# Two attention layers on eight images: the first layer's output projection cut in halves twice and moved behind the next image's queries

## The chip, the cores and the metric

The kernel runs on one core of one Trainium2 chip. The metric is the device time of one execution in microseconds, as the median of several runs. A core has five engines that run side by side, each with its own queue of instructions: TensorE (PE; its weight loads are shown apart as PEld), VectorE (DVE), ScalarE (ACT), GpSimd (POOL) and SyncE (SP), which here does nothing but issue transfers (DMAs) between the chip's DRAM and the on-chip memory, SBUF. TensorE writes its products to another memory, PSUM, from which DVE or ACT must carry them to SBUF ("evict" them). Semaphores hold an instruction until what it needs is there; an engine's queue is worked off strictly in order.

## What is computed

Eight images `x` of 512 channels and 1024 points (32 x 32) go through two attention layers, all in float32. Cut to what matters:

```python
# layer 0: group norm in 32 groups, 8 heads of 64 channels
h = group_norm(x)
q, k, v = split(w_qkv @ h + b_qkv)                 # per head: 64 x 1024 each
weight = softmax((q * s).T @ (k * s))              # s = 64 ** -0.25
a = weight @ v                                     # 512 x 1024
x = x + (w_proj @ a + b_proj)                      # the projection and its residual
# layer 1: group norm in 8 groups, one head of 512 channels
xn = group_norm(x)
q, k, v = q_w @ xn + q_b, k_w @ xn + k_b, v_w @ xn + v_b
attn = softmax(q.T @ k / sqrt(512))
out = x + (p_w @ (attn @ v) + p_b)
```

## The kernel before

**Tiles.** Channels lie on 128 partitions, so an image is four tiles of 128 x 1024. All such tiles (4 KB in each partition) come from one pool, `big`, of `NBIG` = 32; `wpool` holds three sets of weights, loaded a product or two ahead by `load_weight` (line 320) in the order of the list `uses`.

**Fewer multiplications.** A 512 x 512 weight times an image is done as a 2 x 2 block product with seven block products in place of eight (the Winograd form of Strassen's method); this is "in halves once" (`wino`, line 225): sums and differences of the halves of the weights are made in the prologue and kept in DRAM (`prepare`, `keep`), those of the image by `image_factors` (line 343, eight DVE instructions of 128 x 512). "In halves twice" (`conv2`, line 501) does each of the seven block products in seven smaller ones. It needs the weight's inner sums (`keep2`, line 294) and the image's (`inner_factors`, line 403: for each of seven factors four GpSimd subtractions of 128 x 256, in the order of `ORDER`). `conv2` is written as four `pair`s of block products, (1, 5), (2, 6), (7) and (3, 4). Behind each pair the functions in a list of "hooks" are called: this is how other work is placed in the order of the program. The last two steps of a product are put into `tail` and emitted behind the first step of the next one.

**Who uses which.** Values, keys and queries of layer 0 (`values`, `keys_and_queries`) and layer 1's first product (`layer1_scores`, weight "m") are in halves twice; the projection of layer 0 (`projection`, line 954, weight "p") and layer 1's "z" product are in halves once. In `projection` DVE adds bias and residual while it evicts (line 964), half tile by half tile, then the statistics of layer 1's norm are taken (`GroupNorm.half_stats`, line 90) and the result is stored to DRAM (`store`, `spills`).

**The loop** (line 1055) runs over the images b. `attention0` (line 632) has eight blocks, four head pairs `hp` by two halves of the queries `tb`: in each, eight times two score matmuls (`sc`), an exponential on ACT (`e`), DVE adds up the eight exponentials (lines 653 and 655), then 16 matmuls with the values (`av`). Behind each head pair `reciprocals` (line 586) adds the totals over the partitions with TensorE (`sums`), sends them through DRAM and back as a broadcast `r`, by which the result `a` is scaled (line 684) during a later block. The list `extra` has 16 entries, one behind each block's scores and one behind its `av`: work for other engines is hung there. Before the change these are the loads' norm of layer 1 for the image before (`applies`), its halvings, and the halvings of `a`. Then follow the projection of image b, layer 1 of image b - 1 (`layer1_scores`, `layer1_rest`), and the values, keys and queries of image b + 1. The first image has no layer 1 to do yet, the last has no next image.

**Order.** The tile framework orders each engine's instructions by when it reckons them ready, earlier ones in the program first; an instruction given to `tc.keep_in_program_order` stays behind the one traced before it on its engine. All matmuls are pinned in this way, so TensorE works in the order of the program. Other instructions that are ready early may be put ahead.

Of the kernel before, what the change touches and what calls it, by code (L numbers as in the profile page):

```python
# [15 lines left out]
P = 128  # L16
EPS = 1e-5
ORDER = (1, 5, 2, 6, 7, 3, 4)
NBIG = 32
# [10 lines left out]
def two_attention_blocks_kernel(  # L30
# [22 lines left out]
    ident = const.tile([P, P], F32, name="ident")  # L53
    make_identity(nc, ident)
    ones = const.tile([P, P], F32, name="ones")
# [115 lines left out]
    def main_path(ctx):  # L171
# [7 lines left out]
        taken = []  # L179
        spool = ctx.enter_context(tc.tile_pool(name="spill", bufs=2, space=bass.MemoryType.DRAM))  # L180
# [111 lines left out]
        wdram2 = {n: dram.tile([P, 7, 7, P], F32, name=f"sums2_{n}") for n in "qkmv"}  # L292
# [21 lines left out]
        uses = ["p", *layer0] if B > 1 else ["p"]  # L314
        for b in range(1, B):
            uses += ["p", *twice["m"], "z"] + (layer0 if b + 1 < B else [])
# [86 lines left out]
        def inner_factors(hf, uid, pin=lambda ins: ins):  # L403

            f, steps = {}, []
            for p in ORDER:
                t = big_tile(f"inner{p}_{uid}", (P, 4, 2 * P))
                t1, t2, t3, t4 = (t[:, i, :] for i in range(4))
                b11, b12, b21, b22 = (hf[p][k][:, ts(i, 2 * P)] for k in range(2) for i in range(2))
                f[p] = {1: b11, 2: b21, 3: b22, 4: t4, 5: t1, 6: t2, 7: t3}  # L410

                def make(ops=((t1, b12, b11), (t2, b22, t1), (t3, b22, b12), (t4, b21, t2))):
                    for dst, x, y in ops:
                        pin(nc.gpsimd.tensor_tensor(dst, x, y, ALU.subtract))  # L414

                steps.append(make)
            return f, steps
# [168 lines left out]
        def reciprocals(totals, uid, across, direct=None):  # L586
# [8 lines left out]
            for t in range(n):  # L595
                for i in range(4):
                    matmul(
                        sums[ts(i, 32), t, :, :], ones[:, :32], totals[t][:, :, ts(i, P)],
                        start=t == 0, stop=t == n - 1, skip_group_check=True,
                    )  # L600
# [31 lines left out]
        def attention0(b, q, k, v, a, extra):  # L632
            n = 0
            scaled, totals = [], []

            for hp in range(KC):
                for tb in (0, 1) if hp < KC - 1 else (1, 0):
# [35 lines left out]
                    if hp < KC - 1:  # L673
                        if tb == 0:
                            continue
                        dst = a[hp].rearrange("p (t n) -> p t n", t=2)
                    else:
                        dst = dst.rearrange("p (t n) -> p t n", t=1)
                    r = reciprocals(totals, uid, False, nc.scalar if (hp, tb) == (KC - 1, 0) else None)
                    totals = []  # L680
                    engine = nc.gpsimd if (b == 0 or hp == KC - 1) and (hp, tb) != (KC - 1, 0) else nc.vector
                    scaled = [
                        lambda dst=dst, r=r, engine=engine: tc.keep_in_program_order(
                            engine.tensor_tensor(dst, dst, r, ALU.mult)  # L684
                        )
                    ]

            assert not extra
            return scaled[0]
# [118 lines left out]

        def natural(wt, nm, banks):
            ts_ = [pair_tile(f"nat{nm}_{h}") for h in range(2)]  # L810
            t = [ts_[o // 2][:, o % 2, :] for o in range(KC)]
            pt = [ps_tile(banks[o // 2], f"tr_w{nm}_{o}") for o in range(KC)]
            for kc in range(KC):
                for o in range(KC):
                    transpose(pt[o][:, ts(kc, P)], wt[kc][:, ts(o, P)], ident)
            spread(lambda o, copy: tc.keep_in_program_order(copy(t[o], pt[o])), KC)
            return t
# [34 lines left out]
        def prologue():  # L852
            raw_k = raw("k", 5)
# [46 lines left out]
            for n in "pz":  # L900
                t, steps = prepare(n)
                later.append(steps)
                later.append([lambda n=n, t=t: keep(n, t), load_weight])
# [86 lines left out]

        def norm_hooks(norm, uid):

            return [
                [], [all_background], [lambda: norm.group_mean(acc_tile(f"gmean_{uid}")[:, :KC])],
                [lambda: norm.affine(acc_tile(f"gvar_{uid}")[:, :KC])],
            ]
# [11 lines left out]
        def keys_and_queries(b, f, norm, hooks):  # L1008

            mean, affine = [], []  # L1010
            if norm:
                mean.append(lambda: norm.group_mean(acc_tile(f"gmean_0_{b + 1}")[:, :KC]))
                affine.append(lambda: norm.affine(acc_tile(f"gvar_0_{b + 1}")[:, :KC]))
            if hooks:
                k = conv2("k", f, None, f"k0_{b}", hooks)
                q = conv2("q", f, pcols("bq0"), f"q0_{b}", [[all_background], mean, affine])
            else:

                k = conv2("k", f, None, f"k0_{b}", [[all_background, *mean], [], [], affine])
                q = conv2("q", f, pcols("bq0"), f"q0_{b}")  # L1020
            return q, k

        def layer1_scores(b, inner):
            g = conv2("m", inner, ubias, f"g1_{b}")
# [29 lines left out]

        for b in range(B):
# [4 lines left out]
            h, loads, applies = [], [], []  # L1060
            if b > 0:
                h, loads, applies = begun(load_again, norm1, b - 1, "h1")
            elif B > 1:
                h, loads, applies = begun(load_x, norm0, 1, "h0")
            for f in loads:
                f()
            for i, f in enumerate(applies):
                extra[2 * i + 1].append(f)
            a = channel_tiles(f"a0_{b}")

            here = lambda *t: tc.keep_in_program_order(nc.vector.tensor_sub(*t))
            af, steps = image_factors(a, f"a_{b}", here)

            if b > 0:
                hf, t = image_factors(h, f"h1_{b - 1}", here)
                for i, fs in enumerate((t[:1], t[1:2], (t[2], t[4]), (t[6], t[3]), (t[5], t[7]), steps[:2], steps[2:4])):
                    extra[2 * i + 3] += fs
            elif B > 1:
                hf, t = image_factors(h, "h0_1", here)
                for i, fs in enumerate((t[:2], (t[2], t[4]), (t[6], t[3]), (t[5], t[7], *steps[:2]), steps[2:4])):  # L1080
                    extra[2 * i + 7] += fs
            psum_pools(f"attention_{b}", 1)
            scaled = attention0(b, q, k, v, a, extra)
            if B > 1:
                for f in steps[4:7]:
                    f()
            psum_pools(f"products_{b}", 2)
            xt = [load_x(b, c, "x") for c in range(KC)]
            if B > 1:

                inner, sums2 = inner_factors(hf, f"h1_{b - 1}" if b > 0 else "h0_1", tc.keep_in_program_order)
                for f in sums2:
                    f()
                norm1, stats = projection(b, af, xt, [scaled, steps[7]])
            if b > 0:
                gf, gsteps = layer1_scores(b - 1, inner)
                _, _, mean, affine = norm_hooks(norm1, f"1_{b}")
                if b + 1 < B:
                    h, loads, applies = begun(load_x, norm0, b + 1, "h0")
                    ahead, made = factors_ahead(h, loads, applies, f"h0_{b + 1}")  # L1100
                else:
                    h, loads, applies = begun(load_again, norm1, b, "h1")
                    ahead = [loads, *([f] for f in applies)]
                layer1_rest(b - 1, inner, gf, gsteps, stats, [[], mean, [], affine], ahead)
                if b + 1 < B:
                    v, norm0 = values(b + 1, made["inner"])
                    q, k = keys_and_queries(b + 1, made["inner"], norm0, ())
            elif B > 1:
                v, norm0 = values(1, inner)
                hooks = norm_hooks(norm1, "1_0")  # L1110
                hooks[0].append(lambda: background.extend(stats))
                q, k = keys_and_queries(1, inner, norm0, hooks)
            else:
                for f in (*steps[:7], scaled, steps[7]):
                    f()
                all_background()
                norm1, stats = projection(0, af, xt)
                finish()
                background.extend(stats)
                for f in sum(norm_hooks(norm1, "1_0"), []):  # L1120
                    f()
                h, loads, applies = begun(load_again, norm1, 0, "h1")
                for f in loads + applies:
                    f()
# [26 lines left out]
    def general_path(b, ctx):  # L1151
# [6 lines left out]
        wpool = ctx.enter_context(tc.tile_pool(name="gw", bufs=2))  # L1158

# [170 lines left out]
```

## Time and profile before

| | us |
|---|---|
| median of 3 runs (2827.34 to 2829.25) | 2828.92 |
| the profiled execution | 2828.69 |
| its span, first to last instruction | 2826.9 |
| attention of image 4 | 116.8 |
| projection of image 4 (TensorE alone on it) | 24.1 |
| one image, attention to attention | 345.4 |

The projection stands in the profile as the matmuls that write `psa_p`, `psb_p` and `psc_p`; those of the keys as `psa_k` and so on. The groups of the page that bear on the change, with busy time, mean of one, and the idle time of the engine ahead of them:

```
L651 ACT ACTIVATE e<-sc 128x1024 f32<-128x1024 f32 x512 | 476.0, 1054 | 75.8 <-PE sc L62 74.2
L414 POOL TENSOR_TENSOR inner_h<-h,inner_h 128x256 f32<-128x256 f32 x120 | 111.6, 931 | 3.5
L725 POOL TENSOR_TENSOR sum<-sum,e 128x1024 f32<-128x1024 f32 x32 | 76.1, 2378 | 27.4 <-ACT e L721 26.1
```

A matmul appears as two records. The time of a matmul is read from the distance between starts, since consecutive ones overlap. The granted clock of TensorE was 0.999 of full speed.

### The profile page before, as it was taken

Reading aid. Unit: us, or ns where it says so; the run is one execution under the profiler, and the core shown is the slowest. Engines: PE = TensorE matmul, PEld = TensorE weight load, DVE = VectorE, ACT = ScalarE, POOL = GpSimd, SP = SyncE. Lnnn points to the kernel's source line nnn. Section 1 sums busy time; section 2 is a strip of 40 time slices with the busy share of each in tenths; the row PEclk is TensorE's granted clock in tenths of the full one; section 3 lists DMA queues with packets and bytes.
Section 4 is the critical chain, followed back from the end, with each engine's and each line's share of the span. In section 5 each row is a group of like instructions: output and inputs, shape, how many; then the busy total and the mean of one; then the engine's idle time right before and its main releaser. Section 6 shows DMA issues by size and latency. Waiting matters only on the chain.

```text
span 2826.9 us, 33696 instructions
## 1 busy us (share of the span) xinstructions
PE 2808.6 (99%) x12434; PEld 1693.5 (60%) x12434; DVE 2005.0 (71%) x2833; ACT 942.7 (33%) x1205; POOL 1099.4 (39%) x1131
## 2 busy tenths in 40 slices
PE   9999999999999999999999999999999999999998
PEld 5435735866367653677537674376843868338584
DVE  5478677776777767777677766777667776676765
ACT  1252452214522145221552215422154312633130
POOL 2204205841057410664107730177202672036672
PEclk9999999999999999999999999999999999999999
DMA  8634303043031330323212232123311224112301
GB/s 285 209 114 151 147 17 127 27 174 139 24 139 52 147 129 17 139 98 120 110 50 105 101 138 90 53 102 122 140 67 53 102 112 159 36 58 90 119 5 72
DMA packets 107344, 292.41 MB, mean 103 GB/s; under 512 B 19171, under 2 KB 51235, under 8 KB 97446
## 3 DMA queue, kind: packets, MB, share of 16 engines
q1 hardware_dynamic: 105382, 287.92, 28.8%
q10 hardware_dynamic: 1792, 2.29, 0.3%
q8 instruction: 100, 1.64, 0.2%
q14 instruction: 70, 0.57, 0.1%
HBM read 237.47 MB, written 52.70 MB: 103 GB/s over the span
## 4 chain that ended last, share of the span: by engine, by line
PE 96%; DVE 2%; issue 1%; DMA 0%; POOL 0%; ACT 0%; DVEq 0%; ACTq 0%; POOLq 0%
PE sc L62 16%; PE av L62 15%; PE psb_av L62 6%; PE psb L62 5%; PE psa_av L62 4%; PE psc_av L62 4%; PE psc L62 3%; PE psa L62 3%; PE psb_z L62 3%; PE psb_k L62 3%; PE psb_g L62 3%; PE psb_v L62 3%; PE psb_p L62 3%; PE psb_q L62 2%; PE psa_z L62 2%; PE psc_z L62 2%
## 5 line engine op out<-in xcount | busy, mean ns | idle before, releaser
L655 DVE TENSOR_TENSOR sum<-sum,e 128x1024 f32<-128x1024 f32 x384 | 483.9, 1260 | 37.4 <-ACT e L651 0.5
L651 ACT ACTIVATE e<-sc 128x1024 f32<-128x1024 f32 x512 | 476.0, 1054 | 75.8 <-PE sc L62 74.2
L62 PE MATMUL sc<-q,k 64*128 64x512 f32 x2048 | 456.8, 596 | 0.0
L62 PE MATMUL av<-e,v 128*64 128x512 f32 x2048 | 453.6, 595 | 0.0
L684 POOL TENSOR_TENSOR a<-a,r 128x512 f32<-128x512 f32 (+1 forms) x11 | 20.0, 1817 | 903.3 <-DMA r<-all_rows 771.0
L62 PEld LDWEIGHTS sc<-q,k 64*128 64x128 f32 x2048 | 191.6, 186 | 248.0 <-issue 110.6
L62 PEld LDWEIGHTS av<-e,v 128*64 128x64 f32 x2048 | 141.3, 137 | 304.4 <-issue 292.3
L653 DVE TENSOR_TENSOR sum<-e,e 128x1024 f32<-128x1024 f32 x64 | 78.4, 1225 | 166.5 <-ACT e L651 166.5
L669 ACT COPY a<-av 128x512 f32<-128x512 f32 x64 | 37.5, 586 | 321.9 <-PE av L62 321.9
L62 PE MATMUL psb<-inner,inner_h 128*128 128x256 f32 x448 | 116.1, 382 | 0.9
L62 PE MATMUL psa_av<-e,z 128*128 128x512 f32 x256 | 113.3, 595 | 0.0
L414 POOL TENSOR_TENSOR inner_h<-h,inner_h 128x256 f32<-128x256 f32 x120 | 111.6, 931 | 3.5
L135 ACT ACTIVATE h<-h,b,s 128x1024 f32<-128x1024 f32 x62 | 78.5, 1270 | 87.1 <-DMA h<-in_x 69.4
L414 POOL TENSOR_TENSOR inner_h<-h 128x256 f32<-128x256 f32 x60 | 64.6, 1076 | 83.6 <-ACT h L135 83.6
L62 PEld LDWEIGHTS psb<-inner,inner_h 128*128 128x128 f32 x448 | 83.9, 190 | 16.6 <-POOL inner L429 3.5
L462 ACT COPY psb_v<-psa_v 128x512 f32<-128x512 f32 (+1 forms) x28 | 14.5, 517 | 222.4 <-DVE o L785 141.5
L725 POOL TENSOR_TENSOR sum<-sum,e 128x1024 f32<-128x1024 f32 x32 | 76.1, 2378 | 27.4 <-ACT e L721 26.1
L62 PE MATMUL psb_g<-inner_h,w_m 128*128 128x256 f32 x336 | 86.0, 383 | 0.3
L414 POOL TENSOR_TENSOR inner_h<-t_h,inner_h 128x256 f32<-128x256 f32 x90 | 84.2, 935 | 2.4
L414 POOL TENSOR_TENSOR inner_h<-t_h 128x256 f32<-128x256 f32 x90 | 79.9, 894 | 9.7 <-DVE t_h L165 9.7
L62 PEld LDWEIGHTS psa_av<-e,z 128*128 128x128 f32 x256 | 48.0, 190 | 57.3 <-issue 56.6
L721 ACT ACTIVATE e<-e 128x1024 f32<-128x1024 f32 x64 | 65.8, 1053 | 48.5 <-DVE e L711 26.2
(358 smaller groups left out, 5574.8 us busy)
## 6 DMA issues: line engine op xcount, KB each, us to landing
x<-in_x SPq DMA_DIRECT2D x36, 512.0 KB
h<-in_x SPq DMA_DIRECT2D x32, 512.0 KB
r<-all_rows SPq DMA_DIRECT2D x64, 256.0 KB
spill<-x SPq DMA_DIRECT2D x32, 512.0 KB
h<-spill SPq DMA_DIRECT2D x32, 512.0 KB
x<-spill SPq DMA_DIRECT2D x32, 512.0 KB
out<-x SPq DMA_DIRECT2D x64, 256.0 KB
w_p<-sums_p SPq DMA_DIRECT2D x8, 1792.0 KB
```

Source lines behind the costliest of these rows:

```text
L62: tc.keep_in_program_order(nc.tensor.matmul(*args, **kw))
L135: tc.keep_in_program_order(nc.scalar.activation(dst, src, AF.Identity, bias=b, scale=s))
L414: pin(nc.gpsimd.tensor_tensor(dst, x, y, ALU.subtract))
L462: nc.scalar.copy(ps["b"], ps["a"])
L651: nc.scalar.activation(e, sc, AF.Exp, scale=(C // 8) ** -0.5)
L653: nc.vector.tensor_add(total, es[0], e)
L655: nc.vector.tensor_add(total, total, e)
L669: nc.scalar.copy(dst, av)
L684: engine.tensor_tensor(dst, dst, r, ALU.mult)
L721: nc.scalar.activation(e[c, cc, r], e[c, cc, r], AF.Exp, scale=scale)
L725: on = lambda dst, x, y: lambda: tc.keep_in_program_order(nc.gpsimd.tensor_tensor(dst, x, y, ALU.add))
```

## The change

It does the projection of images 0 to 6 with `conv2`, behind the queries of the next image, and only that of image 7 as before.

- `keep2("p")` is added to image 0's attention (four GpSimd operations of 128 x 896, seven stores). `uses` names the two parts of "p" behind each image's queries.
- `attention0` gets a `store`: each head pair's result `a`, once scaled, is stored to DRAM (`kept`), and its tiles come free. The last head pair is then done in the order (0, 1) with one set of sums for both halves, whose matmuls are emitted behind the first step of the next product; GpSimd scales it.
- Four loads `again` bring `a` back behind the second pair of the keys. Behind the last pair of the keys `factors_of_a` begins: eight halvings and 28 inner subtractions on GpSimd, spread over the hooks of the queries and of the projection.
- `projection2` takes the place of `projection`. Bias is added in `conv2`; the residual is four GpSimd additions of 128 x 1024, hung behind the first scores of the next attention (entry 0 of `extra`). Statistics of layer 1's norm stand at entries 1 and 3 (no longer pinned), the store of x at 3, the two small matmuls of the norm at 4 and 5, its application, in place on the tiles of x, at 7 and 9. The load of x that went before (`load_again`, `"h1"`) is gone.
- The halvings of layer 1's input stand at entries 9 to 15, and with each of the last four blocks go the four inner subtractions of one factor, on DVE (`ih[0]` to `ih[3]`); the other three factors stay on GpSimd. Layer 1's first product follows directly on attention.
- `NBIG` is 34 in place of 32; the identity matrix and most of the `ones` leave their constant places.

The diff, cut to its core:

```diff
-NBIG = 32
+NBIG = 34
...
-        uses = ["p", *layer0] if B > 1 else ["p"]
-        for b in range(1, B):
-            uses += ["p", *twice["m"], "z"] + (layer0 if b + 1 < B else [])
+        uses = [*layer0, *twice["p"]]
+        for b in range(1, B - 1):
+            uses += [*twice["m"], "z", *layer0, *twice["p"]]
+        uses += ["p", *twice["m"], "z"]
...
-                    r = reciprocals(totals, uid, False, nc.scalar if (hp, tb) == (KC - 1, 0) else None)
+                    direct = store is None and (hp, tb) == (KC - 1, 0)
+                    engine = nc.gpsimd if (b == 0 or hp == KC - 1) and not direct else nc.vector
+                    scaled = []
+
+                    def scale(hp=hp, dst=dst, totals=totals, uid=uid, direct=direct, engine=engine, scaled=scaled):
+                        r = reciprocals(totals, uid, False, nc.scalar if direct else None)
+                        scaled.append(lambda: tc.keep_in_program_order(engine.tensor_tensor(dst, dst, r, ALU.mult)))
+                        if store:
+                            scaled.append(lambda: store(hp))
+
                     totals = []
+                    if store and hp == KC - 1:
+                        behind.append(scale)
+                    else:
+                        scale()
...
+        def projection2(b, inner, hooks):
+
+            norm = GroupNorm(1, f"1_{b}")
+            y = conv2("p", inner, obias[0], f"p_{b}", hooks)
+            xt = [load_x(b, c, "x") for c in range(KC)]
+
+            def residual(c):
+                nc.gpsimd.tensor_tensor(xt[c], xt[c], y[c], ALU.add)
...
+            stats = [lambda c=c: norm.stats(c, xt[c]) for c in range(KC)]
+            applies = [lambda c=c: norm.apply(nc.scalar, xt[c], xt[c], c) for c in range(KC)]
+            _, _, (mean,), (affine,) = norm_hooks(norm, f"1_{b}")
+            return xt, {
+                0: [lambda c=c: residual(c) for c in range(KC)], 1: stats[:2], 3: [*stats[2:], store], 4: [mean],
+                5: [affine], 7: applies[:2], 9: applies[2:],
+            }
...
+                plan = {
+                    9: [*t[:2], lambda: ih[0](V)], 11: [*t[2:4], lambda: ih[1](V)], 13: [*t[4:6], lambda: ih[2](V)],
+                    15: [*t[6:], lambda: ih[3](V)],
+                }
...
+            kept = apool.tile([KC, P, T], F32, tag="kept", name=f"kept_{b}")
+            scaled, behind = attention0(b, q, k, v, a, extra, lambda hp: nc.sync.dma_start(kept[hp], a[hp]))
+            for f in ih[4:]:
+                f()
+            psum_pools(f"products_{b}", 2)
+            tail.extend(behind)
+            if b > 0:
+                gf, gsteps = layer1_scores(b - 1, inner, [[], scaled])
...
+            else:
+                v, norm0 = values(1, inner, [[], scaled])
...
+                af, t = image_factors(again, f"a_{b}")
+                f, ia = inner_factors(af, f"a_{b}", tc.keep_in_program_order)
+                inner_a.update(f)
+                for f in (*t[:2], ia[0]):
                     f()
...
+                q_hooks[0] += [ia[1]]
+                q_hooks[1] += t[2:4]
+                q_hooks[2] += [ia[2], ia[3]]
+                q_hooks[3] += t[4:6]
+                p_hooks[0] += [ia[4], *t[6:]]
+                p_hooks[1] += [ia[5]]
+                p_hooks[2] += [ia[6]]
+
+            q_hooks, p_hooks = ([[] for _ in range(4)] for _ in range(2))
+            q, k = keys_and_queries(
+                b + 1, inner, norm0, [lambda c=c: load_a(c) for c in range(KC)], [factors_of_a], q_hooks
+            )
+            x1, plan = projection2(b, inner_a, p_hooks)
```

## Prediction, made before the result was known

> **What bounds the kernel now.** I read the page first, then the busy time of each engine by stretch for image 4 (attention begins at 1366.7 us, the next image's at 1712.1), then the order in time of TensorE, VectorE and GpSimd.
>
> ```profile
> PE 2808.6 (99%) x12434; PEld 1693.5 (60%) x12434; DVE 2005.0 (71%) x2833; ACT 942.7 (33%) x1205; POOL 1099.4 (39%) x1131
> PE 96%; DVE 2%; issue 1%; DMA 0%; POOL 0%; ACT 0%; DVEq 0%; ACTq 0%; POOLq 0%
> 1366.70:1483.50 116.80, 116.80 (x578) 43.17 (x577) 84.18 (x82) 68.51 (x76) 5.01 (x4) 1.00 0.15 47
> 1483.50:1527.40 43.90, 43.85 (x150) 27.63 (x147) 31.37 (x50) 7.79 (x14) 27.46 (x35) 1.00 0.39 139
> 1691.00:1712.10 21.10, 21.05 (x97) 17.40 (x95) 13.03 (x31) 6.67 (x11) 5.79 (x9) 1.00 0.71 273
> ```
>
> The first two lines are the page's busy times and chain; the others are stretches (length; then busy time of PE, PEld, DVE, ACT, POOL; clock; DMA share; GB/s): attention, projection with layer 1's first product, queries. TensorE is busy throughout at full clock, so matmul time taken away comes off the end, and only what makes TensorE wait goes back on. In attention VectorE is second (84.2 of 116.8 us) and GpSimd stands almost still (5.0).
>
> **What is removed.** A projection in halves once is 7 x 2 x 2 matmuls of 512 columns, two records each: 56. In halves twice it is 49 of 256 columns: 98 records. The order of TensorE gives both prices:
>
> ```profile
> 1500.74 0.59 PE L62 MATMUL psa_g<-h,w_m 128*128 128x256 f32 x2
> 1501.60 3.60 PE L62 MATMUL psb_p<-t_a,w_p 128*128 128x512 f32 x8
> 1505.03 3.60 PE L62 MATMUL psc_p<-a,w_p 128*128 128x512 f32 x8
> 1669.11 1.03 PE L62 MATMUL psb_k<-inner_h,w_k 128*128 128x256 f32 x4
> ```
>
> Starts are 3.43 us apart for 8 records of 512 columns and 0.87 for 4 of 256 (the next starts at 1669.98). The whole projection runs from 1483.47 to 1500.74 and, after a bit of g, from 1501.60 to 1508.47: 17.27 + 6.87 = 24.14 us. The keys, cut exactly as the new projection, run from 1666.46 to 1691.00 less 1.78 of v, 0.95 of q and 0.28 of norm: 21.53; g gives 21.56 in the same way. I take 21.55. Seven images x 2.59 = **-18.1**. The sums of the last head pair took 0.57 us for each half; together, as for other pairs, 1.00: 7 x 0.14 = **-1.0**. At image 0 the projection's evictions made v wait (0.44 and 0.71 us, 0.16 later) and its first sums waited 1.05 for VectorE: **-2.4** if all of it goes.
>
> **What is added and hidden.** Per image the new projection evicts as queries do (DVE 13.0, ACT 6.7, POOL 5.8 of 21.1 us in the stretch above), beside 8 halvings and 28 GpSimd subtractions of 128x256. Those are 0.93 us each by the inner_h rows (26 us), with 5.8 for each of q and p 37.6 of two products' 43: hidden, with little room. Their DMAs are four stores and four loads of 512 KB on SP; 2 MB at the 273 GB/s of the query stretch is 7.7 us, asked for 12 us into the keys and needed 30 us later. A landing past that lead would be paid in full. The weights grow by one DMA and 1.3 MB, loaded a product ahead as the others are. Sixteen subtractions for layer 1 go from GpSimd to VectorE, four behind each of the last four attention blocks. The nearest row of that width is 0.42 us (an eviction), 1.7 for four; with two halvings (0.69 each) and a scaling (1.22) that is 4.3 of the 4.84 us in which VectorE idles between two blocks' sums. Zero, and up to 0.5 us a time if they cost what halvings cost beside GpSimd (1.1).
>
> **Where TensorE may wait: the residual.** It was on VectorE, reading PSUM. Now it is four GpSimd additions of 128x1024 just behind the projection, hence in the first block of the next attention, where VectorE adds up exponentials.
>
> ```profile
> 1383.88 1.23 DVE L653 TENSOR_TENSOR sum<-e,e 128x1024 f32<-128x1024 f32 x1 [4.84 <-ACT e L651]
> 1385.21 7.87 DVE L655 TENSOR_TENSOR sum<-sum,e 128x1024 f32<-128x1024 f32 x6
> 1392.99 0.69 DVE L1071 TENSOR_TENSOR t_h<-h 128x512 f32<-128x512 f32 x1
> 167.69 9.94 DVE L655 TENSOR_TENSOR sum<-sum,e 128x1024 f32<-128x1024 f32 x6
> 168.86 2.36 POOL L684 TENSOR_TENSOR a<-a,r 128x1024 f32<-128x1024 f32 x1 [50.38 <-DMA r<-all_rows]
> L768 DVE TENSOR_TENSOR t<-e,t x16: 2283/3368/3376, 550.1 to 2761.0; 128x1024 f32<-128x1024 f32 x16
> ```
>
> Six sums take 7.87 us alone and 9.94 with one GpSimd operation among them: it costs VectorE 2.07 of its own 2.36. With GpSimd working likewise (L768) one takes 3.37. They take turns. A block is 14.09 us of TensorE; its sums end 12.3 after its start and the next block's begin at 17.2. After two blocks TensorE reads both totals (the second half a microsecond later); at image 0 a delay of 2.07 cost it 0.1, so the slack is about 2.1. Of the four additions one runs ahead of the sums, one reaches 1.7 into them, two cost 2.07: 5.8 late. Layer 1's statistics now stand behind that block: two channels, four statistics 0.60 apart and two ends of 0.20, 2.8. 5.8 + 2.8 - 4.84 = 3.8 late, a wait of 1.6. Part of the statistics may run while GpSimd holds the sums up, as they read one tensor (0.68 us there too). Bounds for each image: 0 (all fits) and 4.4 (all four channels, 5.6 us, ahead of the second block's sums). I take 1.2, nearer to the order of the code, on images 1 to 7: **+8.4**.
>
> The Trainium skill (SBUF — State Buffer, section "SBUF: two separate sides") speaks against this step: whichever of a VectorE instruction with two SBUF inputs and a GpSimd one starts first holds their shared ports for the whole instruction, and the other blocks. Holding 2.36 instead of the 2.07 seen would make the wait 1.8 to 2.1 us, an estimate by that page, and the sum some 5 us worse; the row decides.
>
> **Smaller waits.** The two tiny norm products move from z into attention; the chain before the second (0.15 + 0.16 + 0.16 + 0.16, in k's stretch) fits the 1.8 us between the sums' end and the block's; where GpSimd works beside it one link is 2.30 us, a wait of 1 us. I take 0, as GpSimd idles there. Eight inner subtractions of h, emitted behind attention but ready before its end, take turns with the last seven sums: 7 x 0.45 (1.17 against 0.72) = 3.2 late, against 1.8 + 0.86 (g's first step now precedes the totals) + 0.5: 0 to 0.3 each, I take **+1.0** for six images; below zero is out, since nothing there shortens TensorE's work. In image 0's attention four GpSimd operations of 128x896 split the projection's factors again: 2.08 us each in the prologue, ready 14.9 us in. Two are past or nearly so when sums begin (1.9 late), two cost 1.85: 5.6 less 2.1, **+3.5**; bounds 0 and 6.
>
> **What else is queued.** On SP the store of x moves from the projection into attention, in front of the first rows: it waits for the residual (some 11 us in), the rows come 29 us in. Each attention result's store waits for its scaling, with only later rows behind it. If rows come late, VectorE stands on their reciprocal with the sums behind it: image 0 shows 4.90 us of that and no wait of TensorE, as another block follows. The last pair's scaling on GpSimd waits for a DMA some 10 us into g, with g's own additions behind it, which before ran 20 us in. Layer 1's activations move to later blocks, two at a time: 2.54 us in the 5 us that ScalarE waits for av.
>
> **Sum.** -18.1 - 1.0 - 2.4 + 8.4 + 1.0 + 3.5 = **-8.6** on the span of 2826.9: 2818.3. The profiled run took 2828.69, 1.8 more, and the median is 2828.92: **2820**.
>
> **Rivals.** *(1) Everything hides.* Statistics that fall behind the second block's sums leave 5.8 - 4.84 = 1.0 late, inside the slack. For it: VectorE idles 28% of attention. Against: all of that idle time lies in pieces of 5 us. -18.1 - 1.0 - 2.4 + 3.5 = -18.0: 2811.
>
> *(2) Slower: VectorE's sums set the first two blocks.* The statistics aren't pinned and are ready early, so all four channels may be ordered into the gap ahead of the second block: 5.8 + 5.6 - 4.84 - 2.1 = 4.4 us in each of seven images, +31 in place of 8.4: +14, 2843. For it: unpinned t_h halvings (L167, L168) run ahead of evictions that stand before them in the code. Against: the second block's sums come first in the code. It decides from 2.4 us a time (17 us over seven images, where the gain is used up), and is slower beyond 0.2% from 3.2.
>
> *(3) The projection waits for its own factors.* GpSimd has 37.6 of 43 us there; if the last four subtractions fall behind the additions of the product before them, TensorE stands some 3 us (two subtractions and what is in front), x 7 = 21: 2820 + 21 = 2841, slower too. Against: they depend on loads long landed and can start ahead.
>
> **How the numbers follow.** 0.2%, 5.7 us, is what a measurement can tell. Forecast 0.43 (2815 to 2826, three quarters of it faster by over 0.2%), rival 1 0.17, rival 2 0.25, rival 3 0.08, an unpriced shortage of tiles or a late load 0.07. Faster 0.32 + 0.17 = 0.49; same 0.11 + 0.04 = 0.15; slower 0.36. The range goes from rival 1 with a little of image 0's waits gone, 2808, to rival 2, 2843.
>
> **What would show it.** TensorE: 98 psx_p records of 256 columns in 21.5 us behind the queries, then sc without a gap. The sums of each first head pair, 28 us into attention, should show a wait for sum L655 of about 1.2 us (0 in rival 1, over 3 in rival 2), and VectorE's first block some 14 us for 7 sums. A wait of psb_p or psc_p for inner_a would be rival 3. I am wrong if the wait sits elsewhere in k, q or p: then the reload or the 34 tiles were underpriced.

## The result, and the profile after

The changed kernel takes 2924.16 us (median of 4 runs, 2917.42 to 2935.51) against 2828.43 for the kernel before on the same chip: ratio 1.0343, 95% interval 1.0310 to 1.0376. It is slower by 96 us, where 2820 was predicted and 2843 was the upper end. The profiled execution took 2924.69, its span is 2922.9 (2826.9 before).

The page's busy times and chain, as shown of before:

```profile
PE 2829.6 (97%) x12728; PEld 1772.7 (61%) x12728; DVE 2053.4 (70%) x3015; ACT 984.0 (34%) x1275; POOL 1302.0 (45%) x1303
PE 83%; DVE 6%; POOL 5%; issue 3%; DMA 3%; ACT 1%; SPq 0%; DVEq 0%; POOLq 0%; ACTq 0%
```

TensorE is busy 21 us longer with matmuls that should take 19 less, and the chain, 96% TensorE before, now runs through VectorE and GpSimd for 11% of the span. The same stretches for the image 4 of before, in the order attention, layer 1's first product, queries, projection (columns as before: length, busy time of PE, PEld, DVE, ACT, POOL, clock, DMA share, GB/s):

```profile
1431.50:1547.90 116.40, 116.40 (x565) 43.33 (x564) 92.68 (x103) 68.08 (x75) 20.20 (x16) 1.00 0.19 62
1547.90:1569.14 21.24, 21.20 (x108) 17.30 (x107) 15.92 (x33) 6.44 (x11) 9.42 (x11) 1.00 0.40 133
1376.60:1398.10 21.50, 21.37 (x99) 18.37 (x98) 14.51 (x34) 5.74 (x10) 13.63 (x20) 1.00 0.42 150
1398.10:1431.50 33.40, 26.76 (x105) 21.28 (x104) 15.65 (x36) 8.60 (x14) 19.25 (x29) 0.90 0.43 160
```

The attention, where I had looked for the loss, is full and no longer than before. The projection, with the end of the queries in it, takes 33.4 us; before, the queries with the end of the keys in them took 23.7 in the same place (1688.3 to 1712.0). TensorE stands 6.6 us in it, and its clock, 1.00 in every stretch of before, is 0.90. The largest waits of TensorE over the whole span (total, times, longest; w_av is a sum that VectorE makes in layer 1's last product, psb without a suffix is a bank of layer 1's scores):

```profile
PE psb_p L60 <- ACT psb_p L462: 30.4, 7, 4.3
PE psb_p L60 <- POOL inner_a L414: 15.5, 7, 2.2
PE sums L60 <- DVE sum L655: 9.6, 3, 5.6
PE psb_av L60 <- DVE w_av L235: 7.5, 2, 3.8
PE psb L60 <- POOL inner L429: 6.3, 6, 1.2
```

With 3.9 us of waits in image 1's values these are 73 us. Two come once in each of the seven moved projections. In TensorE's order they stand here:

```profile
1399.64 0.81 PE L60 MATMUL psb_q<-inner_h,w_q 128*128 128x256 f32 x3
1404.79 2.04 PE L60 MATMUL psb_p<-inner_a,w_p 128*128 128x256 f32 x4 [4.33 <-ACT psb_p L462]
1406.62 1.06 PE L60 MATMUL psa_p<-again,w_p 128*128 128x256 f32 x2
...
1424.59 1.14 PE L60 MATMUL psb_p<-inner_a,w_p 128*128 128x256 f32 x2 [2.21 <-POOL inner_a L414]
```

The second line also shows a loss that no wait accounts for: its four records take from 1404.79 to 1406.62, 1.83 us, where four of this form take 0.87. Around the end of a wait (from 1.9 us ahead of it to 1.4 us behind it) the clock drops to half, for 3.41 or 6.83 us at a time in the record of the granted clock: nineteen such stretches, 78.5 us. They cost at most half of that, 39 us; 7.3 us of them lie inside the waits, so 36 is nearer. Before has none between its first microseconds and its end. 19 us gained on TensorE, 73 lost to waits and 36 to 39 to the clock make +90 to +93 of the 96.0 between the spans.

**The first wait** is read on GpSimd and ScalarE (start, length, instruction, count, idle time before it):

```profile
1394.92 0.72 POOL L535 TENSOR_TENSOR q<-q 128x256 f32<-128x256 f32 x1
1395.60 0.73 POOL L414 TENSOR_TENSOR inner_a<-again 128x256 f32<-128x256 f32 x1
...
1399.14 0.73 POOL L535 TENSOR_TENSOR q<-q 128x256 f32<-128x256 f32 x1
1399.82 0.73 POOL L414 TENSOR_TENSOR inner_a<-t_a,inner_a 128x256 f32<-128x256 f32 x1
...
1401.87 0.73 POOL L535 TENSOR_TENSOR q<-q,q 128x256 f32<-128x256 f32 x1
1402.68 0.72 POOL L535 TENSOR_TENSOR q<-q 128x256 f32<-128x256 f32 x1
```

```profile
1399.91 0.72 ACT L542 ACTIVATE q<-q,par 128x512 f32<-128x512 f32 x1 [5.82 <-POOL q L535]
1403.43 0.72 ACT L542 ACTIVATE q<-q,par 128x512 f32<-128x512 f32 x1 [2.80 <-POOL q L535]
1404.06 0.58 ACT L462 COPY psb_p<-psa_p 128x512 f32<-128x512 f32 x1
```

The eight subtractions for the factors 2 and 6 of the projection (L414, in two runs from 1395.60 to 1401.9) stand in GpSimd's queue ahead of the queries' own last additions (L535), which are needed first. ScalarE works in order: the bias of the queries (L542) waits for those additions, and behind it stands the copy of the projection's first bank (L462), without which TensorE can't begin its next step. Nobody here has too much to do: GpSimd is idle for 7.4 us just before, from 1384.5 to 1391.9. **The second wait** is the same queue the other way round: the last factor's four subtractions follow the projection's additions.

```profile
1422.33 0.72 POOL L535 TENSOR_TENSOR p<-p 128x256 f32<-128x256 f32 x1
1423.01 0.72 POOL L414 TENSOR_TENSOR inner_a<-t_a 128x256 f32<-128x256 f32 x1
...
1425.17 0.72 POOL L414 TENSOR_TENSOR inner_a<-t_a,inner_a 128x256 f32<-128x256 f32 x1
```

### The profile page after: what moved, and what is told of

It reads as the page before. It is cut to its first block, busy times and chain, and to the rows that moved or that the text cites. A ratio compares the mean times of both kernels' runs of the same rounds, so it can differ in the third digit from the quotient of the medians.

```text
span 2922.9 us, 35004 instructions
## 1 busy us (share of the span) xinstructions
PE 2829.6 (97%) x12728; PEld 1772.7 (61%) x12728; DVE 2053.4 (70%) x3015; ACT 984.0 (34%) x1275; POOL 1302.0 (45%) x1303
## 4 chain that ended last, share of the span: by engine, by line
PE 83%; DVE 6%; POOL 5%; issue 3%; DMA 3%; ACT 1%; SPq 0%; DVEq 0%; POOLq 0%; ACTq 0%
PE sc L60 14%; PE av L60 13%; PE psb L60 5%; PE psb_av L60 5%; PE psa_av L60 4%; PE psc_av L60 3%; PE psc L60 3%; PE psa L60 3%; PE psb_z L60 3%; PE psb_k L60 3%; PE psb_p L60 3%; PE psb_v L60 2%; PE psa_z L60 2%; PE psc_z L60 2%; PE psa_k L60 2%
## 5 line engine op out<-in xcount | busy, mean ns | idle before, releaser
L414 POOL TENSOR_TENSOR inner_h<-x 128x256 f32<-128x256 f32 x16 | 15.9, 993 | 337.9 <-PE av L60 337.9
L653 DVE TENSOR_TENSOR sum<-e,e 128x1024 f32<-128x1024 f32 x64 | 90.1, 1408 | 92.2 <-ACT e L651 92.2
L121 POOL TENSOR_TENSOR rstd<-ve,mhalf 128x4 f32<-128x4 f32 x16 | 16.7, 1042 | 280.7 <-DVE ve L119 259.5
L60 PE MATMUL psb_p<-inner_a,w_p 128*128 128x256 f32 x294 | 86.8, 422 | 46.6 <-ACT psb_p L462 30.4
L60 PE MATMUL psb<-inner,inner_h 128*128 128x256 f32 x448 | 116.3, 382 | 6.4 <-POOL inner L429 6.3
L414 POOL TENSOR_TENSOR inner_h<-t_h 128x256 f32<-128x256 f32 x62 | 76.8, 1242 | 63.8 <-DVE t_h L1086 36.9
L60 PEld LDWEIGHTS psb_p<-inner_a,w_p 128*128 128x128 f32 x294 | 58.4, 209 | 66.5 <-POOL inner_a L414 51.3
L685 POOL TENSOR_TENSOR a<-a,r 128x1024 f32<-128x1024 f32 (+1 forms) x11 | 26.4, 2402 | 151.0 <-DMA r<-all_rows 107.9
L462 ACT COPY psb_v<-psa_v 128x512 f32<-128x512 f32 (+1 forms) x28 | 14.5, 517 | 225.3 <-DVE o L792 158.2
L535 POOL TENSOR_TENSOR v<-v,v 128x256 f32<-128x256 f32 x28 | 20.0, 726 | 149.8 <-DVE u_v L530 149.8
L718 DVE TENSOR_TENSOR e<-psc,u 128x512 f32<-128x512 f32 x56 | 38.6, 690 | 68.3 <-PE psc L60 68.3
```

Of the source, the lines that this page charges most:

```text
L60: tc.keep_in_program_order(nc.tensor.matmul(*args, **kw))
L121: nc.gpsimd.tensor_tensor(rstd, ve, mhalf, ALU.pow)
L414: pin(engine.tensor_tensor(dst, x, y, ALU.subtract))
L462: nc.scalar.copy(ps["b"], ps["a"])
L535: nc.gpsimd.tensor_tensor(d, x, y, ALU.add)
L653: nc.vector.tensor_add(total, es[0], e)
```

## The experiments

**x1, x2, x3: the order of GpSimd's queue.** Only the place changes at which the factors are emitted. x1 has the first two lines, x2 the last two, x3 all (several statements are written on one line here).

```diff
-q_hooks[0] += [ia[1]];  q_hooks[1] += t[2:4];  q_hooks[2] += [ia[2], ia[3]]
+q_hooks[0] += [ia[1], ia[2], *t[2:4]];  q_hooks[1] += [ia[3]]
-p_hooks[0] += [ia[4], *t[6:]];  p_hooks[1] += [ia[5]];  p_hooks[2] += [ia[6]]
+p_hooks[0] += [ia[4], *t[6:], ia[5]];  p_hooks[1] += [ia[6]]
```

> The third and fourth factors of the attention result (eight subtractions an image on GpSimd) are emitted behind the queries' first and second pairs, in the stretch where GpSimd stood idle 7.4 us, and no longer ahead of the queries' last additions. Theory A (the order of GpSimd's queue: additions of q late, ScalarE's bias behind them, the projection's first copy behind that): the wait of psb_p for ScalarE's copy, 7 x 4.33 = 30.4 us, goes, and with it the half clock behind it (30.6 us at half, so 15.3): 2924 - 46 = 2878, and the bias of the queries no longer waits for GpSimd. Rival B (the wait comes from ScalarE or the reload, not from GpSimd's order): psb_p still waits about 4 us an image, 2915 to 2925. Rival C (the waits only move on): psb_p's wait goes, but one of the same size appears in the projection's later pairs, 2900 or more.

> The projection's last two factors are emitted one pair earlier, so that the four subtractions of the last stand ahead of the projection's own additions on GpSimd (idle there for 10 us), not behind them. Theory A: the wait of psb_p for inner_a, 7 x 2.21 = 15.5 us, goes with the half clock behind it (7 x 3.4 us at half, 11.9): 2924 - 27 = 2897; the wait for ScalarE's copy stays at 30.4. Rival (the factor is late because its halvings on VectorE are): the wait stays or becomes one for t_a, 2920 to 2925.

> Both moves. Theory A: the sum of the two, 46 + 27 = 73: 2851, with no wait of TensorE above 1 us in the queries and the projection, and a projection of about 21.5 us. What then stays above the kernel before is image 0 (9.6 us of waits for sums, 5 for clock), the two waits for w_av (7.5, and 5 for clock) and the scores (6.3). Rival C: the two waits cover for one another, so that both together bring no more than the larger: 2875 or more.

Measured: x1 2883.79 us (ratio to before 1.0183, 1.0153 to 1.0213), 40 less than the changed kernel where 46 were expected; x2 2900.22 (1.0261, 1.0238 to 1.0283), 24 less for 27; x3 2856.39 (1.0080, 1.0057 to 1.0103), 68 less for 73. Each edit removes its own wait whole and leaves the other: x1 has 15.5 us for inner_a and none for ScalarE's copy, x2 30.5 for the copy and none for inner_a, x3 neither. The largest waits of the three, in this order:

```profile
PE psb_p L60 <- POOL inner_a L414: 15.5, 7, 2.2
```

```profile
PE psb_p L60 <- ACT psb_p L462: 30.5, 7, 4.4
```

```profile
PE psb_av L60 <- DVE w_av L235: 14.0, 4, 3.8
```

Together they bring what they bring apart (40 + 24 = 64), so neither covers the other. In x1 GpSimd's order reads, at the same place:

```profile
1362.73 0.74 POOL L414 TENSOR_TENSOR inner_a<-t_a,inner_a 128x256 f32<-128x256 f32 x1
1364.04 1.41 POOL L535 TENSOR_TENSOR q<-q,q 128x256 f32<-128x256 f32 x2 [0.57 <-DVE u_q L530]
...
1369.20 0.73 POOL L535 TENSOR_TENSOR q<-q 128x256 f32<-128x256 f32 x1
1369.89 0.73 POOL L414 TENSOR_TENSOR inner_a<-again 128x256 f32<-128x256 f32 x1
```

The additions now follow one another and wait only for VectorE. In x1 and x3 the few microseconds short of the expectation go with the wait for w_av, which went from two images to four (7.5 to 14 us); it is the subject of x5 and x8. In x2, 24 for 27 is within the spread of its own runs (2893.59 to 2911.14).

**x4: is the half clock the price of standing still?** Ten matmuls that nothing reads are put where TensorE waited first; the rest is as in the changed kernel.

```diff
+acc = acc_tile(f"filler_{name}")
+for _ in range(10):
+    matmul(acc[:, : 2 * P], weights2[0][:, 0, 0, :], f[1][1], start=True, stop=True)
```

> Ten matmuls of 256 columns (about 4.3 us of TensorE) stand between the projection's first products and the copy that they wait for; their product is read by nothing, everything else is as in the changed kernel. Theory D (the half clock is a price of TensorE's own standing still): the wait of 4.33 us turns into 4.3 us of matmuls, the clock stays at full there, and only the 15.3 us lost to the half clock behind it come off: 2909; the half clock behind the second wait stays. Rival (the half clock comes from the mix of work there, or from a limit on power, whatever TensorE does): the half clock stays in its place, 2920 to 2925. Second rival (the copy is late by TensorE's own progress, so that the wait only follows the filler): the wait stays, 2940 to 2955.

Measured: 2903.45 us (1.0261, 1.0236 to 1.0285), 21 less than without the filler. The first two lines are x4's filler and the 3.4 us behind it, the last one the 3.4 us behind the same wait in the changed kernel (the clock is the third figure from the end):

```profile
1396.00:1400.50 4.50, 4.50 (x21) 3.61 (x19) 1.21 (x3) 1.59 (x3) 4.34 (x7) 1.00 0.75 245
1400.50:1403.90 3.40, 3.34 (x17) 2.98 (x17) 0.00 (x0) 1.65 (x3) 3.32 (x6) 1.00 0.50 215
```

```profile
1404.80:1408.20 3.40, 3.40 (x9) 2.79 (x10) 0.00 (x0) 0.60 (x2) 3.32 (x6) 0.58 0.50 211
```

The projection goes on no earlier, but in the same 3.4 us it does 17 records instead of 9. Keeping TensorE busy with nothing is worth 13 to 15 us here (the half clock at these seven waits took 30.7 us, 4.5 of them inside the waits). The rest of the 21 is not the filler's doing: in the profiled execution only two of the second waits were followed by half clock, against seven (some 8 us less), and one more wait for w_av (10.4 us against 7.5) took part of that back. So a wait of 2.2 us that is followed by half clock costs up to 3.9, and one of 4.33 up to 6.0 or 7.7.

**x7: the residual, the prediction's largest loss.** x7 is x3 with:

```diff
-nc.gpsimd.tensor_tensor(xt[c], xt[c], y[c], ALU.add)
+nc.vector.tensor_tensor(xt[c], xt[c], y[c], ALU.add)
```

> The kernel with both moves of the factors (2856), the residual additions of images 0 to 6 on VectorE instead of GpSimd. The prediction's term (the additions on GpSimd make the first head pair's sums late by 1.2 us in seven images, because the two engines take turns): 8 us less, 2848. Rival (they cost nothing on GpSimd, since the statistics run beside them): no gain; on VectorE four additions of 1.23 and the statistics of 5.6 stand in front of the first block's sums, 10.5 us against some 8.5 now, and sums that now end just in time come up to 2 us late: 0 to 14 more, and half clocks if a wait passes 2 us: 2856 to 2875.

Measured: 2856.79 us (1.0100, 1.0084 to 1.0115), the same as x3. Both scatter with the waits for w_av (x7 2850.76 to 2860.12), so the traces decide: the attentions of images 1 to 6 last 116.7 us with it, 116.3 without (once 116.5). The additions cost TensorE nothing on GpSimd. Why, GpSimd, VectorE and TensorE show in the changed kernel:

```profile
1431.40 9.33 POOL L1012 TENSOR_TENSOR x<-x,p 128x1024 f32<-128x1024 f32 x4 [3.34 <-DVE p L528]
```

```profile
1433.79 1.29 DVE L91 BATCH_NORM_STATS2 bnst<-x 128x6 f32<-128x512 f32 x2 [1.14 <-POOL x L1012]
...
1439.71 2.10 DVE L653 TENSOR_TENSOR sum<-e,e 128x1024 f32<-128x1024 f32 x1
...
1450.58 1.22 DVE L653 TENSOR_TENSOR sum<-e,e 128x1024 f32<-128x1024 f32 x1
1451.90 7.87 DVE L655 TENSOR_TENSOR sum<-sum,e 128x1024 f32<-128x1024 f32 x6
```

```profile
1459.76 1.07 PE L60 MATMUL sums<-sum,ones 128*32 128x256 f32 x16
```

All four channels' statistics do go into the first block, as rival 2 had it, but six of the eight (two for each channel) run while the residual keeps GpSimd busy, to 1440.7. The first block's sums end at 1450.7, the second's at 1459.77. TensorE reads the first of the two totals at 1459.76 and the second half a microsecond later: in time, with half a microsecond to spare.

**x5 and x8: VectorE held by a run of GpSimd.** The wait for w_av in layer 1's last product comes in two images of the changed kernel. VectorE and GpSimd there:

```profile
952.24 7.60 DVE L793 TENSOR_TENSOR o<-o,r 128x512 f32<-128x512 f32 x1
```

```profile
951.74 0.74 POOL L414 TENSOR_TENSOR inner_h<-h,inner_h 128x256 f32<-128x256 f32 x1
952.43 0.73 POOL L414 TENSOR_TENSOR inner_h<-h,h 128x256 f32<-128x256 f32 x1
...
958.57 0.73 POOL L414 TENSOR_TENSOR inner_h<-t_h,inner_h 128x256 f32<-128x256 f32 x1
```

A multiplication that mostly takes 0.69 us lasts 7.60, to half a microsecond after the last of eleven subtractions that follow one another without a gap. x5 and x8 are x3 with the operand left in PSUM, so that VectorE reads one tensor of SBUF:

```diff
-o = upool.tile([P, HT], F32, tag="o", bufs=2, name=f"o_{uid}_{oc}_{c}")
+o = acc_tile(f"o_{uid}_{oc}_{c}") if (row, c) == (1, 1) else ps
...
-nc.vector.tensor_mul(o, o, r[:, c, :])
+nc.vector.tensor_mul(o, ps if u is None else o, r[:, c, :])
```

This is x8; x5 has o = ps throughout, and so overwrites the bank to which one more product is added for the block (0, 1): that block comes out wrong in x5 and in x6, which is built on it. Their instructions are of the same kinds and sizes, and x8 to x10 have the block right.

> The kernel with both moves of the factors (2856), and in layer 1's last product the sum and the scaling by the reciprocals stay in PSUM, so that those VectorE instructions read one tensor of SBUF instead of two; nothing else is changed. Theory L (an instruction of VectorE with two SBUF inputs is held for as long as GpSimd's subtractions follow one another without a gap): no instruction of this product takes more than 1.5 us, the waits for w_av (4 x 3.5 = 14.0) and the half clocks behind them (17 us, so 8.5) go: 2834. Rival (VectorE waits there for something else, a DMA or a busy PSUM bank): instructions of 7 us stay, 2850 to 2860. Rival 2 (PSUM banks come free later and TensorE waits for them instead): new waits of psb_av or psc_av, 2850 or more.

> As the kernel with the last product's sums in PSUM (2836), but where a bank is added to again later the sum goes to a bank of its own. Theory L (VectorE's instructions with two SBUF inputs are held while GpSimd's subtractions run without a gap): again no wait for w_av, 2833 to 2838. Rival (the earlier result came from overwriting that bank, not from the reads): the waits of 3.5 us return in some images, 2845 to 2858.

Measured: x5 2836.05 us (1.0022, 1.0012 to 1.0031), x8 2834.31 (1.0017, 1.0008 to 1.0027). No wait for w_av is left in either, and no instruction of this product is held. The multiplications of that name in the changed kernel, and those that keep it in x8, where the others write back into their bank at a mean of 696 to 700 ns (total and mean ns):

```profile
L793 DVE TENSOR_TENSOR o<-o,r 128x512 f32<-128x512 f32 x48 | 52.4, 1092 | 1.4
```

```profile
L791 DVE TENSOR_TENSOR o<-o,r 128x512 f32<-128x512 f32 x16 | 11.2, 699 | 0.4
```

The spread of the runs goes with it: x3's lie between 2845 and 2859, x8's between 2831 and 2836. What decides whether VectorE is held through the whole run or takes turns with it stays open: sixteen times in the profiles of the changed kernel and x1 to x4 and x7 it was held for 6.9 to 8.1 us, and in the other images of the same kernels the same multiplication took 0.7 to 1.3. In the profile of before none was held.

**x6, x9, x10: the rest.** In image 0's attention SP's queue holds up the first reciprocals: a weight load that waits for its tile stands in front of the read of the rows (the first of the two fences, SP), so VectorE stands 10.69 us with its sums behind (the second), and TensorE then waits 5.61.

```profile
170.63 0.31 SPq L328 DMA_DIRECT2D w_k<-sums_k  x1
170.99 0.43 SPq L615 DMA_DIRECT2D cols<-rows  x1
```

```profile
178.91 0.25 DVE L617 RECIPROCAL recs<-cols 128x16 f32<-128x16 f32 x1 [10.69 <-DMA cols<-rows]
```

x6 is x5 with these places mended:

```diff
-                    later.append([lambda t=t: keep2("p", t)])
-                later[-1].append(load_weight)
+                    again_p = keep2("p", t, apart=True)
...
+                later[5 + 2 * i].append(f)
+            later[14] += [load_weight, load_weight]
...
-engine = nc.gpsimd if (b == 0 or hp == KC - 1) and not direct else nc.vector
+engine = nc.gpsimd if b == 0 and not direct else nc.vector
...
-gf, gsteps = layer1_scores(b - 1, inner, [[], scaled])
+gf, gsteps = layer1_scores(b - 1, inner, [[], [], scaled])
...
+hooks = [[early], hooks[1], stats[:2], stats[2:]]
```

The first lines spread the split over the blocks of image 0's attention and put the weight loads behind the rows. Then the last head pair's scaling goes to VectorE and one pair of products later in g (layer 1's first product), and the last line is the order of the statistics in image 1's values.

> The kernel before this one with the other waits mended: in image 0's attention the four GpSimd operations that split the projection's factors again stand two blocks apart, in pairs, and the weight loads stand behind the reciprocals' rows in SP's queue; image 1's statistics come in the second half of the values; the last head pair's scaling moves from GpSimd to VectorE from image 1 on. Theory (these are the remaining terms: 9.4 for sums and 5.1 for clock in image 0's attention, 7 in its values with 1.7 for clock, 6.3 in the scores): 2834 - 27 = 2807 with 2 or 3 us for new waits, so faster than the kernel before by 0.7%. Rival (the waits move on): 2820 or more.

Measured: 2827.14 us (0.9992, 0.9983 to 1.0001), level with before and 20 worse than expected. Image 0's attention came down from 128.6 us in x3 to 118.5, but the rest moved on, as the rival said: the wait in image 1's values stayed (2.6 us and the clock), the scores waited 4.1 for VectorE instead of 6.0 for GpSimd, and the last image's sums, with its scaling now on VectorE too, came 3.3 late with half clock behind (1.2 without in x5). x9 has x8's banks, takes that scaling back to GpSimd and puts image 2's statistics into image 1's keys:

```diff
+engine = nc.gpsimd if (b == 0 or (hp == KC - 1 and not store)) and not direct else nc.vector
...
+hooks = [late[:2], [*late[2:], *loads], mean, [*affine, *factors]]
```

> The mended kernel (2827) with the same bank of its own; image 2's statistics come in image 1's keys and not in its values; the last image's scalings stay where they were. Theory (what is left there are 3.3 us of wait and 1.7 of clock in the last attention, 5.8 in image 1's values): 2827 - 10 = 2817. Rival (the waits move into the keys): 2825 or more.

Measured: 2818.73 us (0.9962, 0.9948 to 0.9976): faster than both kernels, than the one before by 0.4%. Its largest waits and, for one image, its queries and projection:

```profile
PE sums L60 <- DVE sum L664: 3.4, 3, 2.1
PE psb L60 <- DVE e L727: 3.2, 7, 0.5
```

```profile
1657.60:1679.10 21.50, 21.50 (x100) 18.50 (x99) 15.56 (x35) 6.58 (x11) 20.23 (x28) 1.00 0.41 150
1679.10:1702.80 23.70, 23.60 (x107) 19.58 (x105) 15.97 (x37) 7.96 (x13) 14.61 (x22) 1.00 0.59 225
```

TensorE is busy throughout these two stretches at full clock, with GpSimd at 34.8 of 45.2 us. Of the waits in image 1's values 1.1 us are left; one wait, of 2.1 us in the last image, still has half clock behind it. x10 moves the same scaling from g into z:

```diff
-gf, gsteps = layer1_scores(b - 1, inner, [[], [], scaled])
+gf, gsteps = layer1_scores(b - 1, inner)
...
-layer1_rest(b - 1, inner, gf, gsteps, [], [[]] * 4, ahead)
+layer1_rest(b - 1, inner, gf, gsteps, [], [scaled, [], [], []], ahead)
```

> As the one before, with the last head pair's scaling in z and not in g, where it stood 1.5 us in VectorE's way. Theory: the waits of the scores for VectorE (4.1 us over six images) go, 2813. Rival (tiles held longer stop a load, or z waits instead): 2817 or more.

Measured: 2818.70 us (0.9965, 0.9951 to 0.9979), no gain. The scores wait 3.2 us for VectorE in both, so the scaling was not what they waited for; what it is was not looked for.

## Why the prediction was wrong

**The step that failed** is "What is added and hidden". It set 37.6 us of GpSimd's work against 43 us and called it "hidden, with little room". The load was no problem: a subtraction took 0.73 us, not the 0.93 I took from the inner_h rows, and in x9 the same work fits with 10 us to spare. What I didn't do is put the new instructions into GpSimd's order, hook by hook, next to the additions of the queries and of the projection, and ask of each what would be late behind it. x1 to x3 show it: another order alone took back 68 of the 96 us.

**Rival 3** named one half: the projection's last factor behind additions. It said "some 3 us" seven times and was 2.21. But it said the additions of the product before, it was the projection's own, and the dearer half is the reverse: the factors ahead of the queries' additions, ScalarE's bias behind those, the projection's copy behind the bias. My argument against it, that the factors "can start ahead", doesn't hold in this kernel: `inner_factors` is given `tc.keep_in_program_order` (it stands in the diff), so each factor stays in GpSimd's queue where the hooks put it. Nor was it the reload or the 34 tiles, to which my last line would have put any other wait: x1 removes the first wait and touches neither. Under "What else is queued" I went through SP, the rows and the activations, and left out ScalarE's biases. And 0.08 was too small a chance for the engine with the least room in the sum.

**The clock.** No term of the sum, and no rival, let a wait cost more than its length. Here 73 us of waits cost 36 to 39 more. The trace of before had no wait long enough to show it: behind its first microseconds the longest is 1.05 us. The Trainium skill (TensorE: Matmul & The Clock Gate, section "Part 1: The HAM clock gate (the "warmup" mystery)") has the clock fall to half after an idle window of about 3.4 us; an estimate by that page would have added 1.7 us to each of the 4.33 us waits and nothing to those of 2.21, which in this trace were followed by half clock all seven times; the trace decides.

**The residual, +8.4**: 0 on images 1 to 7, the lower bound that the text gave (x7 and the trace: of the three waits for sums two are in image 0, one at the end of image 7). I let the statistics and the additions follow each other, though the text itself noted that the statistics may run while GpSimd holds the sums up.

**Image 0, +3.5 and -2.4**: four operations that split the factors again made a wait of 2.97 us, as sized, and up to 1.7 of clock. The rows, of which I wrote that a delay there costs TensorE nothing, cost 5.61 and up to 3.4 of clock: the two delays fall on neighbouring head pairs. The waits of image 1's values didn't go, others took their place (3.9); they fell to 1.1 in x9, whose statistics of image 2 no longer stand there.

**Inner subtractions, +1.0**: no wait at the sums, but GpSimd's additions in g came late, behind the scaling, and the scores waited 6.3 in all. I had named the scaling with g's additions behind it, and given it no price.

**The gain was right.** In x9 the round of each of the images 1 to 6, from one attention's first scores to the next's, takes 342.7 to 343.5 us; before it took 345.4. That is 1.9 to 2.7 against the 2.59 + 0.14 predicted, with up to 0.5 us of the new wait of the scores in it. Queries and projection together take the 45.2 us shown, 21.5 more than the 23.7 of the queries before. That x9 comes out at 2819 is no merit of the 2820: the change as it was didn't reach it.

## What to carry to other kernels

When work is moved onto an engine that has room, write down that engine's queue in order and ask of each neighbour who needs it first; the same for every engine that waits for it. A sum of busy times says nothing of this. And price a wait of the matmul engine of 2 us or more at its length and, by these traces, up to 1.7 us of lost clock, up to 3.4 for some of 3.3 us and more.

## What the runs showed that I had not expected

- **How long a wait halves the clock.** Over the twelve profiles, behind the prologue, of 67 waits of TensorE between 0.71 and 1.50 us none was followed by half clock; of 38 between 1.84 and 2.26 us, 22 were; of 48 between 2.6 and 5.9 us, all. It lasts 3.41 us, or 6.83 after 20 of the longer ones. The same wait of 2.21 us does it in one image and not in another, and the record of the clock shows what goes with it: within each profile all these stretches begin whole multiples of 3.413 us apart (to 0.004 us), wherever the waits lie. Cut each of the ten profiles that have any into windows on that grid, and take for each of their 148 waits the most idle time that falls into one window: with 2.0 us or more all 63 were followed by half clock, with 1.83 or less none of 74, between the two 7 of 11. No run moved a wait against the grid on purpose.
- **A hold that outlasts one instruction.** VectorE's multiplication waited for eleven GpSimd instructions, 7.60 us. The Trainium skill (SBUF — State Buffer, section "SBUF: two separate sides") has whichever starts first hold the shared ports for its whole instruction; the multiplications of some 1.15 us agree with that, a hold through a whole run goes beyond it, and there the trace decides.
- **Statistics beside GpSimd.** Instructions that read one tensor ran at their 0.64 to 0.69 us while GpSimd's additions of 2.3 us went on; by the trace, that is what left the residual free.
